# Lower halves of 18 of h's tiles made by TensorE and ScalarE, and another order of work from the sweep's last column to the table of ids

## The chip, the cores and the metric

One core of a Trainium2 chip runs the whole kernel. The metric is the device time of one execution in microseconds (us); the time before is the median of three runs. PE is TensorE (PEld its weight loads), DVE VectorE, ACT ScalarE, POOL GpSimd, SP the engine that only issues transfers.

## The reference

x has 6250 nodes of 256 numbers, and there are 200,000 edges, sorted by their destination. Cut to what matters:

```
deg_out, deg_in = edges per source, edges per destination (at least 1)
h = x * rsqrt(deg_out)
m = segment_sum(h[src], dst) * rsqrt(deg_in)
y = m @ W_gc + b_gc + x @ W_res + b_res
logits = y @ Wg + bg;  the two largest of 64 experts, gates = softmax of the two
per expert: gelu(tokens @ w1 + b1) @ w2 + b2, times the gate, added to y
batch norm over the nodes, added to x, layer norm per node
```

## The kernel before

**Making h.** The source nodes stand in 49 tiles of 128 (hrow). TensorE projects each tile by W_gc first, so that h has 256 columns of x @ W_gc, times the scale s_out of its node. Products of the sweep are done in f32r (one pass), so each row of h is kept in two halves: upper(t) has ScalarE write the scaled row, rounded to f32r, into the tile's first 256 columns; lower(t) has VectorE write what the rounding left, old * s_out - upper, over the unscaled row in the second 256. Each call takes the tiles t-1 and t, t odd. Behind every fourth or sixth tile lower(t) has SP write a block of tiles (512 columns each) to memory as h_dram: the blocks end with the tiles 5, 9, 15, 19, 25, 29, 35, 39, 45 and 48.

**The edge sweep.** The first 1118 groups of 128 edges are taken densely: for each of 30 windows of 128 destination nodes, TensorE counts edges per source and destination (count, L859: one-hot lo of the source by one-hot hotk of the destination, both made by VectorE), ScalarE and VectorE put the counts into SBUF (L879, L902), and multiply (L914, L915) multiplies the counts with the 49 tiles of hrow. The other 445 groups are gathered: GpSimd fetches 128 rows of h_dram by an indirect transfer (fetch, L768) into a ring of 8 buffers, and TensorE adds them by one-hot products (L773, L774). A plan written in advance (dense(), a list of costs) sets the program order: counts of the next window and gathers stand between the multiplies at set distances, and each engine keeps that order. In the opening, 40 groups of the first window are counted with a call of halves(t) after every four; the calls for t = 29 to 49 stand in the first window's multiplies, two tiles apart.

**The sweep's end.** The gathered windows are done before the last dense one, and the last of their results overhangs into the last dense window. last_rows() (L923 to L928) brings it there: after the last multiply ScalarE scales the sum by okc into res (L918), TensorE makes the overhang's product (L926), VectorE adds it (L927), and the ACT queue writes res into z_dram. Meanwhile VectorE works off choices_until(), pieces of the routing of the nodes that are done.

**Routing.** The last three tiles of nodes are loaded from z_dram, finished and sent through the gate; VectorE then ranks each choice within its expert, and TensorE's and VectorE's table() turns the ranks into lists of token ids per expert, by which rows of x are gathered for the experts. busy(n) is n products of TensorE whose result nobody reads. Order is by hand here: `ranks(1, ...)`, then the difference of the two best logits (g2), busy(8), the experts' counts and places (L1479 to L1494, with TensorE's transposition L1486 and product L1487 of them), the table's factors. softmax (L1280) turns g2 into gates: ScalarE's Exp and a copy plus 1, VectorE's reciprocal and two more.

Of the kernel before, what the change touches and what calls it, by code (L numbers as in the profile page):

```python
# [26 lines left out]
TP = 125  # L27
# [23 lines left out]
PAIRS = 8  # L51
MARGIN = 48


# [120 lines left out]
def gnn_moe_kernel(ctx, tc, x_in, x_cols, src, dst, bases, nexts, firsts, parts, lasts, W_gc, b_gc, W_res, b_res, Wg, bg, w1, b1, w2, b2,  # L175
# [9 lines left out]
    def node_rows(ap, t0, n):  # L185
        return ap[t0 * TP:(t0 + n) * TP, :].rearrange("(t p) d -> p t d", p=TP)

    def source_out(tile_ap, ap, t0, n):

        whole = min(n, NS - 1 - t0)  # L190
        if whole > 0:
            nc.sync.dma_start(out=ap[t0 * SP:(t0 + whole) * SP, :].rearrange("(t p) d -> p t d", p=SP),
                              in_=tile_ap[:, :whole, :])
        if t0 + n >= NS:
            for a, b in ((0, 96), (96, ODD)):
                nc.sync.dma_start(out=ap[(NS - 1) * SP + a:(NS - 1) * SP + b, :], in_=tile_ap[a:b, NS - 1 - t0, :])
# [24 lines left out]
    def f32(ap):  # L221
        return ap.bitcast(F32)
# [128 lines left out]
    with tc.tile_pool(name="edges", bufs=1) as ep, ExitStack() as later:  # L351
# [50 lines left out]
        def upper(t):  # L402
            for u in range(t - 1, min(t + 1, NS)):
                S.activation(hrow[:, u, :D], f32(hrow[:, u, D:2 * D]), AF.Copy, scale=s_out[:, u:u + 1])

        def lower(t):
            at = range(t - 1, min(t + 1, NS))
            for u in at:
                V.scalar_tensor_tensor(hrow[:, u, D:2 * D], f32(hrow[:, u, D:2 * D]), s_out[:, u:u + 1],
                                       f32(hrow[:, u, :D]), op0=ALU.mult, op1=ALU.subtract)  # L410
            if t % 5 == 4 or t % 10 == 5:
                n = 6 if t % 10 == 5 else 4
                n -= max(t + 1 - NS, 0)
                t0 = at[-1] + 1 - n
                source_out(f32(hrow[:, t0:t0 + n, :2 * D]), h_dram, t0, n)

        def halves(t):
            upper(t)
            lower(t)

        with tc.tile_pool(name="late", bufs=1) as lp, tc.tile_pool(name="both", bufs=2) as bp, \
# [326 lines left out]
        with tc.tile_pool(name="xs", bufs=1) as xs, tc.tile_pool(name="hotg", bufs=2) as hg, \  # L748
# [6 lines left out]
            for i in range(2):  # L755
                for t0 in range(0, NS, 10):
                    G.memset(f32(counts[i][:, t0:min(t0 + 10, NS), :]), 0.0)

            NR = 8
            ring = []  # L760
# [150 lines left out]
            def multiply(c, t):  # L911

                sm, by = banks[c % 2][:, :D + 2], counts[c % 2][:, t, :]
                T.matmul(sm, by, hrow[:, t, D:], start=(t == 0), stop=False)  # L914
                T.matmul(sm[:, :D], by, hrow[:, t, :D], start=False, stop=(t == NS - 1))  # L915
                if t == NS - 1:
                    res = rsp.tile([WIN, D + 2], F32, name="resd")
                    S.activation(res, sm, AF.Copy, scale=okc[:, c:c + 1])  # L918
                    ends_met["dense"] = res
                    if c < ND - 1:  # L920
                        sums_done(res, c)

            def last_rows():  # L923

                pw, res = banks[(ND - 1) % 2][:, :D + 2], ends_met["dense"]
                T.matmul(pw, live["overd"], ends_met["gather"], start=True, stop=True)  # L926
                V.tensor_tensor(res, pw, res, ALU.add)  # L927
                sums_done(res, ND - 1, ACT_E, nc.scalar)  # L928

# [126 lines left out]
            def dense():  # L1056
# [21 lines left out]
                for c in range(ND):  # L1078
# [10 lines left out]
                    for t in range(NS):  # L1089
# [14 lines left out]
                        if c == ND - 1:  # L1104
                            if t == NS - 6:
                                yield 0.0, lambda: live.update(overd=rows_of(ND, "overd"))
                            yield 0.0, lambda t=t: choices_until(0.25 * t)

# [35 lines left out]
            def gather(n):  # L1144
                i, g = rows[n]
                g0, k = GATHER[i]
                if g == g0:
                    live["pg"] = ps_g.tile([WIN, D + 2], F32, name="pg")
                hot, further = batch.pop(n)
# [32 lines left out]
            for n in range(n, len(rows)):  # L1182
                gather(n)
            last_rows()
            choices_until(1e9)
# [93 lines left out]

    def softmax(g1, g2):  # L1280
        S.activation(g2, g2, AF.Exp)
        S.activation(g1, g2, AF.Copy, bias=1.0)
        V.reciprocal(g1, g1)
        V.tensor_mul(gates[:, :, 1], g2, g1)
        V.tensor_copy(gates[:, :, 0], g1)
# [18 lines left out]
    with tc.tile_pool(name="ps_r", bufs=1, space=PSUM) as ps_r, tc.manual_schedule():  # L1304
# [4 lines left out]
        brow = rt.tile([E, H + D], F32, name="brow")  # L1309
        nc.sync.dma_start(out=brow[:, :H], in_=b1)  # L1310
        nc.sync.dma_start(out=brow[:, H:], in_=b2)
        for t0 in range(ta, tb, 4):
# [6 lines left out]
        for t0 in range(0, NL, 4):  # L1319
            n = min(4, NL - t0)  # L1320
            node_dma(nc.sync, True, z[:, t0:t0 + n, :], node_rows(z_dram, ta + t0, n))
        pick[1] = [rt.tile([TP, E, NB], BF16, name=f"pick{j}") for j in range(2)]
        both[1] = rt.tile([TP, E, NB], BF16, name="both")
# [153 lines left out]
        V.tensor_sub(g2, top[:, :, 1], top[:, :, 0])  # L1477
        busy(8)
        V.tensor_copy(own, cps[:E, 3, 1:2])  # L1479
# [345 lines left out]
    with tc.For_i(0, n_again, 1), tc.tile_pool(name="all", bufs=1) as ap, \  # L1825
# [115 lines left out]
        g2 = ap.tile([TP, NT], F32, name="g2")  # L1941
        V.tensor_sub(g2, top[:, :, 1], top[:, :, 0])
        softmax(g1, g2)
        nc.sync.dma_start(out=node_rows(x_dram[:, D:], 0, NT), in_=gates)
# [236 lines left out]
```

## Time and profile before

| | us |
|---|---|
| runs | 1441.87, 1441.97, 1438.64 (median 1441.87) |
| profiled execution | 1442.04 |
| its span in the trace | 1440.4 |
| busy: TensorE, VectorE, ScalarE, GpSimd | 1334.3 (93%), 1079.3 (75%), 803.4 (56%), 758.1 (53%) |

The span in 40 slices of 36 us; a digit is the busy share in tenths, PEclk the clock that TensorE was granted, in tenths of 2.4 GHz, DMA the share of the 16 DMA engines:

```
PE   8999578999999999999999998799999999999683
DVE  9999889999989888777777768655555555544588
ACT  7898646577776666656555532533333333333358
POOL 6000337777667776766777643255465556565100
PEclk9999699999999999999999999899999999999897
DMA  6667676777778787778788764789788888687645
```

Slice 5 (144 to 180 us) is the end of the projections and the opening of the sweep, slices 25 and 26 (864 to 936 us) hold the sweep's end and the routing. Behind them come the 64 experts, and from about 1340 us the norms.

### The profile page before, as it was taken

How to read it: one execution, taken by the hardware profiler on the slowest of the kernel's cores; microseconds unless marked ns; L12 is line 12 of the kernel's file. 1: busy time of each engine (PE TensorE's matmuls, PEld its weight loads, DVE VectorE, ACT ScalarE, POOL GpSimd, SP SyncE). 2: the span in 40 equal slices, each digit the busy share in tenths (PEclk: the TensorE clock that was granted, in tenths of full speed). 3: DMA queues.
4: the chain of work that ended last, by engine and by line, in shares of the span. 5: the costliest groups of instructions: out<-in, count | busy, mean ns of one | idle time of the engine just before them, and what ended most of it. 6: DMA issues, size and time to landing. Idle time of an engine off the chain costs nothing. (4 is left out here: it accounts for less than half of the span.)

```text
span 1440.4 us, 32497 instructions
## 1 busy us (share of the span) xinstructions
PE 1334.3 (93%) x9814; PEld 1121.1 (78%) x9814; DVE 1079.3 (75%) x3326; ACT 803.4 (56%) x2127; POOL 758.1 (53%) x894
## 2 busy tenths in 40 slices
PE   8999578999999999999999998799999999999683
PEld 4555367888889999999999996688788998799441
DVE  9999889999989888777777768655555555544588
ACT  7898646577776666656555532533333333333358
POOL 6000337777667776766777643255465556565100
PEclk9999699999999999999999999899999999999897
DMA  6667676777778787788778764789788888687645
GB/s 213 192 206 221 223 244 180 208 227 217 206 223 228 211 234 221 216 227 228 218 214 229 208 189 137 170 237 300 258 274 280 257 253 261 212 266 237 248 142 168
DMA packets 198010, 319.89 MB, mean 222 GB/s; under 512 B 27345, under 2 KB 129595, under 8 KB 197826
## 3 DMA queue, kind: packets, MB, share of 16 engines
q1 hardware_dynamic: 149716, 170.68, 38.2%
q0 software_dynamic: 47888, 146.88, 35.4%
q8 instruction: 79, 1.29, 0.4%
q14 instruction: 105, 0.86, 0.2%
q10 hardware_dynamic: 222, 0.19, 0.0%
HBM read 250.84 MB, written 60.35 MB: 216 GB/s over the span
## 5 line engine op out<-in xcount | busy, mean ns | idle before, releaser
L768 POOL DMA_INDIRECT r<-h_dram,srcg x445 | 470.5, 1057 | 215.9 <-PE pc L859 70.6
L914 PE MATMUL sm<-hrow,room 128*128 128x258 f32 x1470 | 486.8, 346 | 5.2 <-DVE room L902 5.0
L879 ACT CAST room<-pc 128x196 f32 (+7 forms) x879 | 356.5, 406 | 163.2 <-PE pc L859 125.2
L915 PE MATMUL sm<-hrow,room 128*128 128x256 f32 x1470 | 394.7, 282 | 0.0
L859 PE MATMUL pc<-hotk,lo 128*128 128x245 bf16 (+7 forms) x1118 | 302.6, 303 | 24.0 <-DVE lo L386 12.9
L837 DVE TENSOR_TENSOR hotk<-key,iota_h 128x784 bf16<-128x784 f16 (+4 forms) x488 | 247.8, 508 | 96.1 <-PE pc L859 91.3
L914 PEld LDWEIGHTS sm<-hrow,room 128*128 128x128 f32 x1470 | 287.5, 196 | 12.4 <-issue 7.3
L915 PEld LDWEIGHTS sm<-hrow,room 128*128 128x128 f32 x1470 | 279.7, 190 | 1.2
L1674 ACT ACTIVATE hT<-ph,bc 128x112 f32<-128x112 f32 (+16 forms) x256 | 108.3, 427 | 257.9 <-PE ph L1672 252.7
L902 DVE TENSOR_TENSOR room<-pc,room 128x49 f32 x908 | 197.5, 240 | 12.5 <-ACT room L879 5.5
L1672 PE MATMUL ph<-xgT,w1s 128*128 128x112 f32 (+17 forms) x1024 | 201.5, 341 | 0.5 <-DVE xgT L1655 0.4
L1630 POOL DMA_INDIRECT y_dram<-ys,dest x124 | 120.0, 968 | 138.9 <-ACT ys L1726 100.1
L1672 PEld LDWEIGHTS ph<-xgT,w1s 128*128 128x128 f32 x1024 | 166.8, 193 | 20.1 <-issue 2.3
L1630 POOL DMA_INDIRECT xg<-x_dram,ids x124 | 120.4, 971 | 62.5 <-DMA w1s<-in_L_gnn_w_dram 21.4
L859 PEld LDWEIGHTS <-lo 128*128 128x128 bf16 x1118 | 97.9, 100 | 62.6 <-DVE lo L386 14.3
L773 PE MATMUL pg<-r,hot 128*128 128x258 f32 x445 | 143.2, 322 | 3.5 <-DMA r<-h_dram,srcg 1.8
L774 PE MATMUL pg<-r,hot 128*128 128x256 f32 x445 | 125.2, 281 | 0.0
L1688 PE MATMUL py<-w2s,hT 128*128 128x256 f32 (+3 forms) x424 | 103.0, 386 | 0.9 <-DVE y_sum L1727 0.9
L1655 DVE TENSOR_SCALAR xgT<-pte,bsum 128x112 f32<-128x112 f32 (+14 forms) x128 | 48.7, 422 | 70.2 <-PE pte L1652 69.8
L611 PE MATMUL pr<-room,f 128*128 128x512 f32 x196 | 99.6, 633 | 0.0
L1710 PE MATMUL ph<-hT,w2s 128*128 128x208 f32 (+9 forms) x480 | 98.1, 358 | 0.0
L386 DVE TENSOR_TENSOR lo<-lo_b,iota 128x1024 bf16<-128x1024 bf16 x140 | 95.9, 685 | 0.0
(374 smaller groups left out, 1942.6 us busy)
## 6 DMA issues: line engine op xcount, KB each, us to landing
w1s<-in_L_gnn_w_dram SPq DMA_DIRECT2D x64, 512.0 KB
w2s<-in_L_gnn_w_dram SPq DMA_DIRECT2D x64, 512.0 KB
yr<-y_dram SPq DMA_DIRECT2D x10, 1024.0 KB
h_dram<-hrow SPq DMA_DIRECT2D x5, 1536.0 KB
r<-h_dram,srcg POOLq DMA_INDIRECT x445
f<-in_x_cols_dram SPq DMA_DIRECT2D x25, 256.0 KB
z_dram<-zeros SPq DMA_DIRECT2D x7, 903.0 KB
r_dram<-hx SPq DMA_DIRECT2D x24, 256.0 KB
```

The lines of the kernel that those rows point to most:

```text
L768: G.indirect_dma_start(out=f32(r[:, :2 * D]), out_offset=None, in_=h_dram[:, :], in_offset=bass.IndirectOffsetOnAxis(ap=idx, axis=0))
L773: T.matmul(pg, hot, r[:, D:], start=first, stop=False)
L774: T.matmul(pg[:, :D], hot, r[:, :D], start=False, stop=last)
L837: V.tensor_tensor(hot, pairs(key, e, n, m), iota_h[:, None, :m, :].to_broadcast([128, n // 2, m, 2]), ALU.is_equal)
L859: T.matmul(pc, los[g // PAIRS][:, r // 2, :, r % 2], hots.pop(g), start=(i == 0), stop=(i == k - 1))
L879: put = S.copy(counts[c % 2][:, :, 1:][:, :, ds(at, w - 1)], pc[:, :, 1:])
L902: add = V.tensor_tensor(to, more, f32(had), ALU.add).ins
L914: T.matmul(sm, by, hrow[:, t, D:], start=(t == 0), stop=False)
L915: T.matmul(sm[:, :D], by, hrow[:, t, :D], start=False, stop=(t == NS - 1))
L1630: w = G.indirect_dma_start(**kw)
L1672: T.matmul(ph[:, :m], w1s[:, kk, c * 128:(c + 1) * 128], xgT[:, kk, :m], start=(kk == 0), stop=(kk == 1))
L1674: S.activation(hT[:, c, :m], ph[:, :m], AF.Gelu, bias=b1_e[:, c:c + 1])
```

## The change

- Every odd tile from 5 to 39 (18 of them, TURNED) gets its lower half in another way. lower(t) has ScalarE make a diagonal matrix of the tile's scales (the identity times s_out, two buffers). At the next call of halves, TensorE multiplies it with the unscaled rows (f32, into half of a PSUM bank) and subtracts the upper half with a product by the constant -1 diagonal (f32r). At the call behind that, ScalarE copies the result to the lower half. The write of a block waits until none of its tiles is under way (rows_to_dram). The bank is the one that the gathers use later.
- The overhang's product (met_rows) is made three tiles before the sweep's end into the other sum bank, and ScalarE copies it to SBUF. After the last multiply one VectorE instruction, sum * okc + overhang, takes the place of ScalarE's scaling, the product and the addition.
- The loads of b1 and b2 (128 and 64 KB) are issued behind those of z_dram's last rows and not ahead of r_dram's.
- Exp and the copy plus 1 (powers) are issued behind `ranks(1, ...)`, ahead of the counts; the rest of softmax stays. busy(8) there becomes busy(2).

```diff
+TURNED = range(5, 40, 2)
...
+        ahead, outs, low = [], [], {}
+
+        def by_products():
+            for u, done in list(ahead):
+                at = low["bank"][:, u // 2 % 2 * D:u // 2 % 2 * D + D]
+                if done:
+                    S.activation(hrow[:, u, D:2 * D], at, AF.Copy)
+                    ahead.remove((u, done))
+                else:
+                    T.matmul(at, low.pop(u), f32(hrow[:, u, D:2 * D]), start=True, stop=False)
+                    T.matmul(at, low["less"], hrow[:, u, :D], start=False, stop=True)
+                    ahead[ahead.index((u, done))] = (u, True)
+
+        def rows_to_dram():
+            while outs and all(u >= sum(outs[0]) for u, done in ahead):
+                t0, n = outs.pop(0)
+                source_out(f32(hrow[:, t0:t0 + n, :2 * D]), h_dram, t0, n)
+
         def lower(t):
             at = range(t - 1, min(t + 1, NS))
             for u in at:
+                if u in TURNED:
+                    low[u] = low["pool"].tile([128, 128], F32, name="scales", bufs=2)
+                    S.activation(low[u], ident, AF.Copy, scale=s_out[:, u:u + 1])
+                    ahead.append((u, False))
+                    continue
                 V.scalar_tensor_tensor(hrow[:, u, D:2 * D], f32(hrow[:, u, D:2 * D]), s_out[:, u:u + 1],
                                        f32(hrow[:, u, :D]), op0=ALU.mult, op1=ALU.subtract)
             if t % 5 == 4 or t % 10 == 5:
...
-                source_out(f32(hrow[:, t0:t0 + n, :2 * D]), h_dram, t0, n)
+                outs.append((t0, n))
+            rows_to_dram()
 
         def halves(t):
+            by_products()
             upper(t)
             lower(t)
...
+            low["pool"] = xs
+            low["bank"] = ps_g.tile([128, 2 * D], F32, name="pg")
+            low["less"] = xs.tile([128, 128], F32R, name="less")
+            S.activation(low["less"], ident, AF.Copy, scale=-1.0)
...
                     res = rsp.tile([WIN, D + 2], F32, name="resd")
-                    S.activation(res, sm, AF.Copy, scale=okc[:, c:c + 1])
-                    ends_met["dense"] = res
                     if c < ND - 1:
+                        S.activation(res, sm, AF.Copy, scale=okc[:, c:c + 1])
                         sums_done(res, c)
-
-            def last_rows():
-
-                pw, res = banks[(ND - 1) % 2][:, :D + 2], ends_met["dense"]
+                    else:
+                        V.scalar_tensor_tensor(res, sm, okc[:, c:c + 1], live["met"], op0=ALU.mult, op1=ALU.add)
+                        sums_done(res, c, ACT_E, nc.scalar)
+
+            def met_rows():
+                assert made["gathered"] == 0
+                met = xs.tile([128, 4 * TP], F32, name="xT", bufs=1)[:, :D + 2]
+                pw = banks[ND % 2][:, 512 - (D + 2):]
                 T.matmul(pw, live["overd"], ends_met["gather"], start=True, stop=True)
-                V.tensor_tensor(res, pw, res, ALU.add)
-                sums_done(res, ND - 1, ACT_E, nc.scalar)
+                S.copy(met, pw)
+                live["met"] = met
...
+                            if t == NS - 3:
+                                yield 0.0, met_rows
...
-            last_rows()
...
-    def softmax(g1, g2):
+    def powers(g1, g2):
         S.activation(g2, g2, AF.Exp)
         S.activation(g1, g2, AF.Copy, bias=1.0)
+
+    def softmax(g1, g2):
         V.reciprocal(g1, g1)
...
-        nc.sync.dma_start(out=brow[:, :H], in_=b1)
-        nc.sync.dma_start(out=brow[:, H:], in_=b2)
         for t0 in range(ta, tb, 4):
             n = min(4, tb - t0)
             node_dma(nc.sync, True, x(t0, n), node_rows(r_dram, t0, n))
...
             node_dma(nc.sync, True, z[:, t0:t0 + n, :], node_rows(z_dram, ta + t0, n))
+        nc.sync.dma_start(out=brow[:, :H], in_=b1)
+        nc.sync.dma_start(out=brow[:, H:], in_=b2)
...
         V.tensor_sub(g2, top[:, :, 1], top[:, :, 0])
-        busy(8)
+        powers(g1, g2)
+        busy(2)
```

## Rows read from the trace of the kernel before

**Rows 1.** Stretches: us, busy us (instructions) by engine, granted clock, DMA share, GB/s.
```profile
155.00:175.00 20.00, 5.58 (x45) 3.40 (x43) 19.03 (x49) 14.47 (x42) 7.18 (x23) 0.67 0.82 302
```
**Rows 2.** VectorE in order of time: start us, us, engine, line, operation, how many.
```profile
165.07 0.60 DVE L837 TENSOR_TENSOR hotk<-key,iota_h 128x882 bf16<-128x882 f16 x1
165.60 0.86 DVE L409 SCALAR_TENSOR_TENSOR hrow<-hrow,s_out 128x256 fp32r<-128x256 f32 x2
...
168.07 0.60 DVE L837 TENSOR_TENSOR hotk<-key,iota_h 128x882 bf16<-128x882 f16 x1
...
181.58 0.88 DVE L409 SCALAR_TENSOR_TENSOR hrow<-hrow,s_out 128x256 fp32r<-128x256 f32 x2
```
**Rows 3.** GpSimd in order of time, the first gather; in brackets its wait.
```profile
199.02 1.09 POOL L768 DMA_INDIRECT r<-h_dram,srcg  x1 [35.91 <-DMA h_dram<-hrow]
```
**Rows 4.** Stretches of the writes of h, with all engines.
```profile
181.80:183.40 1.60, 1.54 (x15) 1.29 (x13) 1.60 (x6) 1.43 (x5) 0.00 (x0) 1.00 0.02 6
183.40:196.70 13.30, 8.87 (x54) 7.23 (x52) 11.89 (x34) 6.50 (x23) 0.00 (x0) 0.74 1.01 369
```
**Rows 5.** Stretches, the gathers of line 768 alone: GpSimd, clock, DMA.
```profile
199.00:287.00 88.00, 69.52 (x60) 1.00 0.68 193
```
**Rows 6.** Waits of TensorE, 250 to 300 us: total us, times, longest.
```profile
PE pg L773 <- DMA r<-h_dram,srcg: 1.8, 2, 0.9
```
**Rows 7.** ScalarE in order of time, a call of halves in the opening.
```profile
159.50 0.91 ACT L404 ACTIVATE hrow<-hrow,s_out 128x256 fp32r<-128x256 f32 x2
160.31 0.23 ACT L879 CAST room<-pc 128x49 f32 x1
160.39 0.52 ACT L404 ACTIVATE hrow<-hrow,s_out 128x256 fp32r<-128x256 f32 x1
```
**Rows 8.** Groups by line, whole span: count, busy us, mean ns, idle before.
```profile
L1162 ACT COPY resg<-pg 128x258 f32<-128x258 f32 x28 | 10.5, 376 | 12.4 <-PE pg L1160 11.5 <-PE pg L774 0.6 <-issue 0.3
L1137 ACT CAST hot<-thin 128x128 fp32r<-128x128 bf16 x44 | 10.2, 295 | 14.4 <-DVE thin L386 14.3
```
**Rows 9.** TensorE in order of time, f32 products of 256 columns (experts).
```profile
931.56 1.96 PE L1688 MATMUL py<-w2s,hT 128*128 128x256 f32 x8
```
**Rows 10.** TensorE in order of time, the sweep's last products.
```profile
869.86 0.28 PE L914 MATMUL sm<-hrow,room 128*128 128x258 f32 x1
869.98 0.28 PE L915 MATMUL sm<-hrow,room 128*128 128x256 f32 x1
870.83 0.70 PE L926 MATMUL sm<-resg,overd 128*128 128x258 f32 x2 [0.57 <-ACT resd L918]
```
**Rows 11.** VectorE in order of time, the same moment.
```profile
871.02 0.53 DVE L343 TENSOR_TENSOR room<-room 125x704 bf16<-125x704 bf16 x1
871.57 0.43 DVE L927 TENSOR_TENSOR resd<-sm,resd 128x258 f32<-128x258 f32 x1
```
**Rows 12.** Waits, 869 to 925 us: total us, times, longest.
```profile
DVE s_in L1417 <- DMA room<-z_dram: 1.3, 1, 1.3
```
**Rows 13.** VectorE in order of time, the experts' places.
```profile
890.06 0.07 DVE L1483 DVE_READ_ACCUMULATOR scr<-haves,place,ones 64x1 f32 x1
...
892.71 0.29 DVE L1493 CAST place_b<-cps 125x128 f16<-125x128 f32 x1 [1.45 <-PE cps L1487]
```
**Rows 14.** TensorE in order of time, the same stretch.
```profile
889.44 2.56 PE L1398 MATMUL acc_c<-room 125*125 125x352 bf16 x8
891.92 0.37 PE L1486 MATMUL cps<-ident,first_b 64*128 64x64 f32 x1
```
**Rows 15.** ScalarE in order of time, ahead of the gates.
```profile
898.57 1.28 ACT L1281 ACT_TABLE_LOAD   x1
```
**Rows 16.** VectorE in order of time, the gates.
```profile
900.41 0.47 DVE L1283 RECIPROCAL g<-g 125x50 f32<-125x50 f32 x1 [0.25 <-ACT g L1282]
```
**Rows 17.** Stretch of 1 us, TensorE alone: busy us, clock, DMA share, GB/s.
```profile
891.00:892.00 1.00, 1.00 (x5) 0.50 1.09 345
```

More of the change, by code (lines that the diff above doesn't have):

```diff
@@ L414, in lower @@
                 t0 = at[-1] + 1 - n
-                source_out(f32(hrow[:, t0:t0 + n, :2 * D]), h_dram, t0, n)
+                outs.append((t0, n))
+            rows_to_dram()
         def halves(t):
+            by_products()
             upper(t)
             lower(t)
+            assert t < NS - 1 or not ahead
         with tc.tile_pool(name="late", bufs=1) as lp, tc.tile_pool(name="both", bufs=2) as bp, \
@@ L1147, in gather @@
                 if g == g0:
-                    live["pg"] = ps_g.tile([WIN, D + 2], F32, name="pg")
+                    live["pg"] = ps_g.tile([WIN, 2 * D], F32, name="pg")[:, :D + 2]
                 hot, further = batch.pop(n)
@@ L1942, in gnn_moe_kernel @@
         V.tensor_sub(g2, top[:, :, 1], top[:, :, 0])
+        powers(g1, g2)
         softmax(g1, g2)
```

## The prediction, made before the changed kernel ran

> **What bounds the kernel now.** By the page's table of engines TensorE is nearly full, so a change to VectorE's work counts only where TensorE isn't. The 40 slices show two such stretches that the change touches: the opening of the edge sweep and the routing behind it. The table by stretches is next: from 155 to 175 us TensorE works 5.6 of 20 us, at 0.67 of its clock, and VectorE 19.0 [rows 1]. The order of VectorE's instructions says on what: one period of the opening, from one one-hot instruction to the next, is 3.00 us and holds two calls of halves, with four lower halves, 0.86 us a pair [rows 2]. So VectorE paces the making of h, at 1.50 us a call.
>
> It is tempting to stop there, but GpSimd's order names a second bound. Its first row gather waits 35.9 us, for the last write of h to memory, and starts at 199.0 us [rows 3]. These writes fill the DMA engines at 369 GB/s to 196.7 us; the one sizeable hole, 181.8 to 183.4, is one in which no block was ready [rows 4]. From then on GpSimd is full: between 199 and 287 us it starts 60 gathers, 69.5 us busy; with the 0.30 us that it stands between two of them that is 87.5 of 88 [rows 5]. And TensorE waits there for gathered rows, 1.8 us [rows 6]. So at 287 us the sweep stands where this rigid chain lets it: landing of h plus 60 gathers. A sweep that comes sooner waits longer; only h landing at another time, or a sweep later by over some 2 us, moves that point. Behind it TensorE is full to the sweep's end and again in the experts, so a shift there, or in the routing, goes through to the end.
>
> **Lower halves.** VectorE loses 18 instructions, 18 x 0.43 = 7.7 us. For each of them ScalarE gets a scaled identity (128x128) and a copy of 256 columns out of PSUM, TensorE an f32 and an f32r product.
>
> ScalarE's old work in a call is two upper halves, which the next instruction follows after 0.81 us, and half of the period's two count copies, 0.08 us each to the next start: 0.89 us at most [rows 7]. The nearest row to the new copy is the 258-column one, 0.38 us, some 0.10 less back to back (two of 0.52 us end after 0.91) [rows 7, 8]. A scaled identity is not in the trace; it lies between the 128x128 cast, 0.29 alone and 0.20 in a run, and the 256-column one with a scale, 0.40 [rows 7, 8]; I take 0.28. Sum: 0.89 + 0.28 + 0.28 = 1.45 us back to back, 1.55 if the copy starts from a wait; bounds 1.35 and 1.70. I take 1.50. So ScalarE takes VectorE's place at the same pace, and VectorE's 7.7 us become waiting: it can't run ahead, since the even tile's lower half needs the upper half that ScalarE makes in the same call. The Trainium skill (ScalarE: Activation LUTs, What ACT_TABLE_LOAD costs) gives 186 ns and 0.83 ns a column, 93 ns more for a scale by pointer, 93 ns of overlap: estimates of 0.31 and 0.29 us for the two, by which the sum would be 1.49.
>
> TensorE's f32 product of 256 columns is two instructions of 0.245 us, the f32r one follows at 0.12: 0.61 us, at the lower clock up to 1.22 [rows 9, 10]. With a call's four counts that fits into 1.50 us at 2.4 GHz and about fills it at 1.2. Free while the clock holds; up to 0.2 us a call if not.
>
> What moves is the landing of h: a block of tiles now waits for its last odd tile, whose copy stands two calls later at the head of ScalarE's work. ScalarE was in the call of tile 9 at 159.5 us [rows 7]; two scaled identities and the constant -1 one put that to 160.3. The block that ends with tile 35, the one behind the hole, is then ready 15 calls later: 160.3 + 15 x 1.50 + 0.33 = 183.1 us. Before, VectorE had its last pair done at 182.46 [rows 2]. The shift is +0.7 us, and the 13.3 us of full DMA behind it hand it on to the first gather. At 1.35 us a call it is -1.6, though the holes allow no more than -0.8 (below), at 1.70 +3.7. I take +0.7. The blocks are alone in SP's queue then, and the PSUM bank is the gathers', whose first product comes later.
>
> **Sweep's end to ids.** The chain was: last matmul done at 870.26, ScalarE's scaling, the f32 product of the overhanging rows (0.70 us), VectorE's addition, done at 872.00 [rows 10, 11]. Now the product stands three tiles ahead of the end, and one VectorE instruction scales and adds. That looks like a cut of over 1 us, but VectorE was not free: an addition of the choices ran to 871.55, and that of res began at 871.57 [rows 11]. The new instruction stands behind the same choices and is about as long. Gain 0.0; bounds +0.6, if the choices come earlier, and -0.3, for the product between TensorE's last tiles. GpSimd's constants waited for ScalarE's scaling, the last reader of okc, and now wait for VectorE's instruction; all that they can hold up is ranking, which VectorE's wait for z hides.
>
> b1 and b2 (192 KB) behind z instead of ahead: they shared the engines with the write of res for which z's load waits. Only VectorE's wait for z, 1.3 us, can be gained [rows 12]. I take 0.4, bounds 0 and 0.8. They are read behind the last tiles' choices, long after.
>
> Six fillers less: the eight took 2.56 us, and the transposition behind them started at 891.92 though its operand was there at 890.13. VectorE waited 1.45 us for it, from 891.26 on [rows 13, 14]. Two fillers, 0.64 us at the rate of the eight, let the transposition and the product behind it end near 891.0, before VectorE is free. Gain 1.45 us; bounds 0 (third rival) and 1.45.
>
> The exponential ahead: its table load, 1.28 us, moves to where ScalarE waits for the counts, and VectorE's reciprocal no longer waits 0.25 us [rows 15, 16]. With the gap ahead of the reciprocal I take 0.35, bounds 0.2 and 0.4.
>
> **Sum.** +0.7 - 0.0 - 0.4 - 1.45 - 0.35 = -1.5 us. The profiled execution took 1442.04 us (span 1440.4), 0.17 above the median of the runs, 1441.87; on that the forecast is 1440.4 us, and the rivals below count from it too.
>
> **Clock.** Under the eight fillers the granted clock was 0.50 with TensorE always busy [rows 17]. The Trainium skill (TensorE: Matmul & The Clock Gate, Part 1) calls the throttled state the default, which activity releases. By that rule less filling can hold the lower level longer; no row here shows the leaner stretch, so it is the third rival.
>
> **Rivals.**
> 1. Faster: the hole of 1.6 us closes, since the calls take 1.45 us or less and the products keep the clock up. The blocks start 0.8 later, so h lands 0.8 sooner; with 0.8 for b1 and b2, 1.45 and 0.4 that is -3.45, 1438.4 us, and 1437.0 where the choices also gain 0.6 and the sweep 0.8. For it: TensorE idles through most of the opening. Against: ScalarE's sum.
> 2. Slower: ScalarE and TensorE in lock-step. The copy waits for a product, the product for ScalarE's identity, the next count copy for counts queued behind that product. At 1.8 us a call tile 35 is ready at 187.6, 5.2 us late; less 2.2 that is +3.0, 1444.9 us; at 1.9, 1446.3. It decides from 1.6 us a call, where h's loss passes the gain behind the sweep. For it: at the lower clock TensorE fills a call. Against: five count banks and two identities let each run somewhat ahead.
> 3. The clock stays low behind the fillers: the products of the places outlast VectorE and the 1.45 us are lost, 1441.8 us.
> 4. The first gather is not held by h's last write, or not the sweep by the gathers: VectorE's 7.7 us come through, within TensorE's 14 idle us. Then 1441.9 - 7.7 - 2.2 = 1432.0 us. The wait of 35.9 us speaks against it.
>
> **How the numbers follow.** Forecast 0.47, rival 1 0.22, rival 2 0.18, rival 3 0.09, rival 4 0.04. A measurement of this kernel can tell 0.3% (4.3 us) from no change. Faster by that, below 1437.5: half of rival 1, rival 4, a little of the forecast: 0.2. Slower by that, above 1446.2: some two thirds of rival 2, at 1.9 us and more a call: 0.12. Within it 0.68. The range, 8 in 10, is 1436.5 to 1445.5; the forecast's own is 1439.0 to 1442.5.
>
> **What would show it.** Right: 31 lower halves on VectorE, which idles for ScalarE in the opening; a first gather between 199 and 201; GpSimd as full to 287 us as before, with TensorE waiting longer for rows; the write of res no nearer to the last tile's choices; no wait of VectorE for the transposed counts and no table load behind them. Wrong: a first gather before 198, a sweep that ends 3 us sooner, calls above 1.6 us, or the clock at its lower level through the places.

## The result: slower, 1467.16 us

Forecast 1440.4 us. Measured: median 1467.16 us (1462.20 to 1467.49, five runs) against 1441.87 (1438.64 to 1444.58, five runs): ratio 1.0174, 95% interval 1.0160 to 1.0187. The profiled execution has a span of 1465.7 us, before 1440.4: +25.3 us.

| | before | after |
|---|---|---|
| first write of h issued | 159.69 | 163.20 |
| first gather | 199.02 | 223.57 (+24.55) |
| 9th, 61st, 201st, 441st gather | 210.20, 287.27, 489.90, 843.01 | +26.05, +26.40, +27.13, +27.12 |
| last product of the sweep starts | 869.98 | 897.68 (+27.70) |
| from there to the end of the span | 570.4 | 568.0 (-2.4) |

So the loss is complete when the gathers start, and goes to the end nearly as it is; behind the sweep the sum comes near the forecast's, though its pieces do not (below). First, GpSimd's order at its first gather [rows 3]:

```profile
start us, us, engine line op out<-in xcount [idle before <-releaser]
223.57 1.31 POOL L799 DMA_INDIRECT r<-h_dram,srcg  x1 [61.54 <-DMA h_dram<-hrow]
```

It waits for h 25.6 us longer. The stretch of the opening [rows 1]:

```profile
core 0: us, PE busy (x) PEld busy (x) DVE busy (x) ACT busy (x) POOL busy (x), PEclk, DMA share, GB/s
155.00:175.00 20.00, 11.06 (x43) 7.03 (x42) 9.90 (x23) 11.99 (x38) 7.03 (x23) 0.59 0.46 170
```

TensorE works twice as long as before, at a lower clock, VectorE half as long, and the DMA engines are at 0.46. No engine is full: engines wait for each other. Of before's VectorE period [rows 2] this is left, one call of halves on all engines (TensorE's weight loads left out):

```profile
165.11 0.24 ACT L910 CAST room<-pc 128x49 f32 x1 [0.85 <-PE pc L890]
165.20 0.39 ACT L413 ACTIVATE hrow<-pg 128x256 fp32r<-128x256 f32 x1
165.48 0.91 ACT L405 ACTIVATE hrow<-hrow,s_out 128x256 fp32r<-128x256 f32 x2
165.65 1.22 PE L416 MATMUL pg<-hrow,scales 128*128 128x256 f32 x2 [0.63 <-ACT hrow L413]
166.02 0.48 DVE L433 SCALAR_TENSOR_TENSOR hrow<-hrow,s_out 128x256 fp32r<-128x256 f32 x1 [0.40 <-ACT hrow L405]
166.27 0.40 ACT L430 ACTIVATE scales<-ident,s_out 128x128 f32<-128x128 f32 x1
166.31 0.78 PE L417 MATMUL pg<-hrow,less 128*128 128x256 f32 x1
...
166.88 0.55 PE L890 MATMUL pc<-hotk,lo 128*128 128x98 bf16 x4
167.53 0.24 ACT L910 CAST room<-pc 128x49 f32 x1 [0.86 <-PE pc L890]
167.62 0.39 ACT L413 ACTIVATE hrow<-pg 128x256 fp32r<-128x256 f32 x1
...
168.07 1.22 PE L416 MATMUL pg<-hrow,scales 128*128 128x256 f32 x2 [0.63 <-ACT hrow L413]
```

Read it as a ring. ScalarE's copy of a tile starts (165.20); 0.45 us later the f32 product of the next tile starts, which waited for that copy though it writes the other half of the bank; the two products take 1.23 us, the four counts behind them 0.65; then ScalarE's copy of the counts, and 0.09 us later, behind it in ScalarE's order, the copy of that tile (167.62). Once round is 2.42 us. TensorE's part of it is long too: the two products take 1.23 us from the first's start to the counts, and 0.66 in two_banks below, where the granted clock is 1.00 (2.4 GHz). Here it is 0.50 (1.2 GHz) from 158.8 to 213.4 us; the table by stretches in the middle of that:

```profile
175.00:190.00 15.00, 11.61 (x44) 8.02 (x44) 7.21 (x18) 9.31 (x30) 0.00 (x0) 0.50 0.60 230
```

In the first window four multiplies come into the ring, mostly 3.36 us a call. The waits of 155 to 215 us say the same (engine and line, what it waited for, us in total, times, the longest):

```profile
DVE hrow L433 <- ACT hrow L405: 21.6, 18, 2.8
ACT room L910 <- PE pc L890: 19.5, 17, 2.0
PEld pg L416 <- ACT hrow L413: 15.9, 17, 1.5
PE pg L416 <- ACT hrow L413: 11.4, 17, 1.2
...
ACT less L789 <- DMA hrow<-hx: 2.9, 1, 2.9
```

17 of the 18 products wait for the copy before. The last line is another cost: ScalarE stands 2.9 us ahead of making the constant -1 identity, for the transfer of projected rows (hx), which by this releaser still reads the place where the constant lies.

The Trainium skill (PSUM — Partial Sum Buffer, PSUM bank collisions raise a hardware error) says that two engines may not use one PSUM bank in the same partitions at the same time, whatever the addresses, and that a program's semaphores are to guard PSUM by bank and not by address. The trace agrees: TensorE's write to one half waits for ScalarE's read of the other, 17 times of 18. This rule speaks against the change, and the forecast didn't weigh it. The runs don't tell whether the wait hangs on the bank or on the tile of the program that fills it, since two_banks below gives each half a tile and a bank of its own.

### The profile page after: what moved, and what is told of

The parts are those of the page before. It is cut to its first block, busy times and chain, and to the rows that moved or that the text cites. A ratio compares the mean times of both kernels' runs of the same rounds, so it can differ in the third digit from the quotient of the medians.

```text
span 1465.7 us, 32612 instructions
## 1 busy us (share of the span) xinstructions
PE 1359.4 (93%) x9862; PEld 1138.7 (78%) x9862; DVE 1074.6 (73%) x3308; ACT 815.6 (56%) x2164; POOL 756.1 (52%) x894
```

## The experiments

Openings start at slightly different times from execution to execution (after: TensorE's clock over 150 to 155 us was 0.80, before 0.50), so the landing of h is counted from ScalarE's first upper halves (four in one row) to the first gather. ScalarE's order in the kernel before, and in the changed one:

```profile
155.70 1.71 ACT L404 ACTIVATE hrow<-hrow,s_out 128x256 fp32r<-128x256 f32 x4
```

```profile
154.14 1.71 ACT L405 ACTIVATE hrow<-hrow,s_out 128x256 fp32r<-128x256 f32 x4
```

With [rows 3] that is 199.02 - 155.70 = 43.32 us, and 223.57 - 154.14 = 69.43: the loss is 26.1 us, 1.56 of it covered by an earlier start. For all kernels (ratios to the kernel before on the same chip, whose median is in the last column):

| kernel | starts | first gather | landing | ratio, 95% interval | before |
|---|---|---|---|---|---|
| before | 155.70 | 199.02 | 43.32 | | |
| the change | 154.14 | 223.57 | 69.43 | 1.0174 (1.0160 to 1.0187) | 1442 |
| early_only | 156.26 | 224.59 | 68.33 | 1.0154 (1.0118 to 1.0190) | 1547 |
| gap_filled | 155.94 | 210.99 | 55.05 | 1.0107 (1.0072 to 1.0141) | 1530 |
| gap_filled_early | 155.92 | 210.34 | 54.42 | 1.0089 (1.0060 to 1.0117) | 1547 |
| copy_first | 155.47 | 208.48 | 53.01 | 1.0103 (1.0061 to 1.0145) | 1530 |
| two_banks | 154.80 | 204.75 | 49.95 | 1.0090 (1.0056 to 1.0124) | 1529 |
| two_banks_early | 154.73 | 203.66 | 48.93 | 1.0039 (1.0014 to 1.0065) | 1530 |
| nine_tiles | 155.96 | 205.81 | 49.85 | 1.0045 (1.0025 to 1.0064) | 1547 |
| doubled | 155.68 | 210.38 | 54.70 | 1.0059 (1.0041 to 1.0076) | 1442 |
| dead_products | 155.49 | 201.87 | 46.38 | 1.0030 (1.0007 to 1.0054) | 1529 |
| ends_only | 154.84 | 200.99 | 46.15 | 1.0022 (1.0004 to 1.0040) | 1529 |
| left_out | 155.22 | 198.95 | 43.73 | | |
| five_tiles | 154.12 | 197.61 | 43.49 | 0.9973 (0.9963 to 0.9983) | 1442 |
| three_tiles | 155.40 | 197.97 | 42.57 | 0.9997 (0.9983 to 1.0010) | 1442 |
| ends_clean | 155.82 | 199.14 | 43.32 | 0.9992 (0.9970 to 1.0014) | 1530 |
| eight_fillers | 155.73 | 199.05 | 43.32 | 0.9993 (0.9978 to 1.0007) | 1442 |

The chips differ (last section), so landings are compared across them and whole times only within one. The kernel before and the two that have neither turned tiles nor the constant (ends_clean, eight_fillers) land at 43.32, to the hundredth, where the whole takes 1440 us and where it takes 1528.

**ends_only: the way behind the sweep alone.**

```
-TURNED = range(5, 40, 2)
+TURNED = ()
```

> The lower halves all on VectorE again, the new way behind the sweep kept. If the loss lies only in the making of h: first gather of rows within 0.3 us of 199.0, the stretch from the sweep's last product to the end as in the changed kernel, 2.1 us shorter than before (570.1 to 568.0 us), so 1441.9 - 2.1 = 1439.8 us. Rival, that part of the loss is behind the making of h (the product of the overhanging rows among the last tiles, or the later writes): first gather at 199, but 1441.5 us or more.

The landing is not as before but 2.8 us later. ScalarE's order names it:

```profile
154.84 1.71 ACT L405 ACTIVATE hrow<-hrow,s_out 128x256 fp32r<-128x256 f32 x4
156.45 0.56 ACT L645 COPY hx<-pr 128x512 f32<-128x512 f32 x1
159.92 0.31 ACT L789 ACTIVATE less<-ident 128x128 fp32r<-128x128 f32 x1 [2.91 <-DMA hrow<-hx]
```

The constant is still made, and holds the next upper halves until the transfer of hx is done.

**two_banks.**

```
-at = low["bank"][:, u // 2 % 2 * D:u // 2 % 2 * D + D]
+at = low["bank"][u // 2 % 2][:, :D]          # the gathers' bank, and the second window's
```

> The two places for the products lie in two PSUM banks, not in two halves of one. Theory (the shared bank ties TensorE's next product to ScalarE's copy of the tile before, with the counts between them): the wait for that copy goes, a call of the opening takes what TensorE needs at 1.2 GHz, 0.66 + 0.57 + 0.62 = 1.85 us instead of 2.42, and one of the first window 2.69 instead of 3.37; 13 x 0.57 + 8 x 0.68 = 12.8 us come back, 1454 us; if TensorE without gaps is granted 2.4 GHz as well, ScalarE's 1.55 us sets the call, and 25 us come back, 1442. Rival (ScalarE's order, the count's copy ahead of the tile's copy, makes the lock-step, whatever the bank): 2.3 us a call or more, 1464 us or more.

The landing comes back by 19.5 us of 26.1. A call takes 1.45 us in the opening, and the clock is up from 166.4 us on. All engines in the opening, weight loads left out, and a stretch:

```profile
168.24 0.24 ACT L911 CAST room<-pc 128x49 f32 x1
168.32 0.40 ACT L413 ACTIVATE hrow<-sm 128x256 fp32r<-128x256 f32 x1
168.39 0.70 PE L416 MATMUL pg<-hrow,scales 128*128 128x256 f32 x2 [0.88 <-ACT scales L430]
168.59 0.91 ACT L405 ACTIVATE hrow<-hrow,s_out 128x256 fp32r<-128x256 f32 x2
168.74 0.47 PE L417 MATMUL pg<-hrow,less 128*128 128x256 f32 x1
169.05 0.36 PE L891 MATMUL pc<-hotk,lo 128*128 128x98 bf16 x4
...
169.39 0.41 ACT L430 ACTIVATE scales<-ident,s_out 128x128 f32<-128x128 f32 x1
...
169.68 0.25 ACT L911 CAST room<-pc 128x49 f32 x1
```

```profile
175.00:190.00 15.00, 11.52 (x81) 9.10 (x78) 10.48 (x26) 13.65 (x45) 0.00 (x0) 1.00 0.81 303
```

(The second is the table by stretches; ScalarE is the fourth engine, the granted clock the third number from the end.) No product waits for a copy; ScalarE goes from one round to the next without a gap, 0.08 + 0.27 + 0.80 + 0.29 = 1.44 us. That is the forecast's sum back to back (0.89 + 0.28 + 0.28). The whole is 13.8 us slower than before on this chip (8.6 to 19.0), more than the 6.6 us of landing explain: in the profiled executions, 7.4 us lie behind the start of the sweep's last product (611.5 us to the end, 604.1 in ends_only), where both run the same code. two_banks_early's 5.6 us of landing below are 6.0 us of the whole.

**left_out and dead_products: the room, and the load.** left_out has nothing in place of the 18 lower halves. dead_products keeps VectorE's, and does products that nobody reads:

```
+T.matmul(at, ident, f32(hrow[:, 1, D:2 * D]), start=True, stop=False)
+T.matmul(at, low["less"], hrow[:, 1, :D], start=False, stop=True)
```

> The lower halves of the 18 tiles are left out altogether (those columns keep what they held), with nothing on TensorE and ScalarE in their place: what the change could at best give. Theory (h's writes fill the DMA engines, and gathers follow at their own pace): VectorE needs 2.14 instead of 3.00 us for two calls, but h lands at most 1.6 us sooner, the hole closed; first gather 197.4 to 199.0, 1439.8 less 0 to 1.6: 1438.2 to 1439.8 us. Rival (VectorE's 7.7 us come through to the end): 1432 us.

> VectorE makes all lower halves as before; TensorE does 18 pairs of products of the same size at the same places in its order, on a finished tile, and nobody reads them: TensorE's load without the ties. By the ties alone (theory): VectorE sets the call at 1.50 us again, first gather at 199 to 201 us, 1440 to 1442 us. By TensorE's load at 1.2 GHz alone (rival): its 1.85 us a call in the opening and 2.69 in the first window hold the counts, and through them VectorE; first gather at 205 us or later, 1448 us or more.

Both still make the constant, so ends_only is their measure. left_out lands 2.4 us sooner than that: all that VectorE's 7.7 us can be worth here. (Its h is not right, its later stages work on other data, and the whole takes 13036 us; only its opening is read.) dead_products lands 0.23 us later: TensorE's added products cost next to nothing by themselves. What cost 26 us is ScalarE's added work and, above all, how it and the products are tied.

**ends_clean and two_banks_early: without the constant's wait.**

```
-low["less"] = xs.tile([128, 128], F32R, name="less")
+low["less"] = ep.tile([128, 128], F32R, name="less")    # made earlier; in ends_clean not at all
```

> All lower halves on VectorE and the constant -1 identity gone too; only the new way behind the sweep is left. Theory: ScalarE's wait of 2.9 us for the transfer of hx, which it had in the changed kernel and with the ends alone (it makes the constant in a place that this transfer still reads), goes; the first write of h is issued at 159.7 us again and not at 161.7, the first gather starts 2.0 us sooner than with the ends alone, at 199.0, and the whole is 2.1 us faster than the kernel before (ratio 0.9985). Rival (that wait was hidden behind the transfers, and the ends alone are what lost): first write at 159.7, first gather at 201 all the same, ratio 1.000 or more.

> Two PSUM banks for the products, and the constant -1 identity made earlier, in a place of its own. Theory: ScalarE sets the call at 1.45 us as with two banks alone, the start comes back by 2.0 us; first gather at 204.75 - 2.0 = 202.7 us, 3.7 us later than before, less 2.1 us behind the sweep: ratio 1.001. Rival (the start is hidden, the landing follows from ScalarE's work alone): first gather at 204.5, ratio 1.002 or more.

ends_clean lands at 43.32 as before: the wait was 2.8 us of landing. With two banks only 1.0 us comes back, for the first scaled identity then waits for the same transfer, 2.1 us. What is left, 5.6 us: the first write is issued 7.98 us behind the start, before 3.99; the rest are calls of 1.5 to 2.3 us in the first window.

**gap_filled: one bank, and dead products in the gaps.**

```
+for n in range(3):
+    T.matmul(low["spare"][:, :D], low["less"], hrow[:, 1, :D], start=True, stop=True)
 T.matmul(at, low.pop(u), f32(hrow[:, u, D:2 * D]), start=True, stop=False)
```

> One bank with two halves as in the changed kernel; ahead of each f32 product TensorE does three dead products of 256 columns into the other window's bank, 0.64 us at 1.2 GHz, as long as the gap in which it waits for ScalarE's copy. Theory (the gaps that the tie leaves keep the granted clock at 0.50, and half of the loss is that): the clock rises to 1.0 within some us, a call takes copy 0.45 + products 0.65 + counts 0.36 + the count's copy 0.15 = 1.6 us in the opening and 2.0 in the first window; first gather at 203 to 206 us, 1446 to 1449 us by the first comparison's chip. Rival (the tie alone makes the 2.42 us, or dead products lengthen the loop): clock 0.50, 2.4 us a call or more, first gather at 223 us or later, 1467 us or more.

One turn of the ring, and the same stretch:

```profile
170.60 0.39 ACT L413 ACTIVATE hrow<-pg 128x256 fp32r<-128x256 f32 x1
170.88 0.91 ACT L405 ACTIVATE hrow<-hrow,s_out 128x256 fp32r<-128x256 f32 x2
171.05 0.70 PE L418 MATMUL pg<-hrow,scales 128*128 128x256 f32 x2 [0.21 <-ACT hrow L413]
171.40 0.46 PE L419 MATMUL pg<-hrow,less 128*128 128x256 f32 x1
...
171.70 0.37 PE L893 MATMUL pc<-hotk,lo 128*128 128x98 bf16 x4
...
171.89 0.60 PE L417 MATMUL sm<-hrow,less 128*128 128x256 f32 x3
172.16 0.25 ACT L913 CAST room<-pc 128x49 f32 x1
172.26 0.39 ACT L413 ACTIVATE hrow<-pg 128x256 fp32r<-128x256 f32 x1
```

```profile
175.00:190.00 15.00, 12.67 (x90) 10.11 (x88) 9.59 (x25) 12.46 (x41) 0.00 (x0) 1.00 0.87 325
```

The ring is the same, more work is in it, and it turns in 1.65 us, since the clock is 1.00: 14.4 us of landing for nothing but dead work (the first gather was expected 5 us sooner still; the first window takes 2.2 us a call, and the clock rose only at 168.1 us). That it is the clock, and not the filling by itself, is seen in the calls before that, TensorE's order:

```profile
162.58 1.22 PE L418 MATMUL pg<-hrow,scales 128*128 128x256 f32 x2 [0.20 <-ACT scales L432]
...
164.15 0.99 PE L417 MATMUL sm<-hrow,less 128*128 128x256 f32 x3
165.03 1.22 PE L418 MATMUL pg<-hrow,scales 128*128 128x256 f32 x2
```

At 0.50 and without a gap a call still took 2.45 us (and the next 2.41). So over half of the loss is the clock, which in the changed kernel stayed at 0.50 with TensorE at work for 63 to 89% of each 5 us and a gap of mostly 0.63 to 0.69 us in each call; the wait for the bank at the full clock is 5.1 us more (gap_filled to two_banks). The Trainium skill (TensorE: Matmul & The Clock Gate, A second HAM failure mode: psum-queue depth-cycling) tells of a kernel whose short idle times between groups of products take the clock down and up over and over. This case differs: with such gaps the clock stayed down for 55 us here, and in two_banks it stayed at 1.00 with a gap of 0.44 us in each call of 1.45. There it had risen at 166.4 us, behind calls with gaps of 0 to 0.19 us. Which gaps keep it down, no run shows.

**copy_first: the tile's copy ahead of the count's copy.**

```
+if g % 4 == 3:                     # and ahead of the counts in the first window
+    yield 0.0, lambda: copies()
 yield of_one_hots(0) / n, lambda g=g: count(g)
```

> One bank with two halves; ScalarE's copy of a tile is put ahead of the count's copy in its order, and so no longer waits for the four counts that TensorE does behind that tile's product. Theory (the tie costs this much only since the copy stands behind the counts; TensorE needs 1.85 us at 1.2 GHz without gaps): the wait for the copy before goes, the clock rises, ScalarE sets the call at 1.45 to 1.55 us; first gather at 203 to 206 us. Rival (the halves of one bank tie product and copy in any order): 2.0 us a call or more, first gather at 215 us or later.

In between: mostly 1.97 us a call while the clock was low (TensorE waits 0.18 us for the copy, the copy 0.33 for the product), about 1.45 once it rose at 172 us, 1.9 to 3.0 when it was at 0.50 again from 179 to 186, and 3.1 us later in landing than two banks. The order was a part of it, but not the whole.

**The last of the ring: gap_filled_early and early_only**, both with the constant made early.

> One bank, the gaps filled with dead products, and the constant made early. Theory (what the first gather gains passes to the end one to one while it is later than in the kernel before): granted clock 1.0 in the opening, 1.65 us a call, first gather at 209 to 210 us, 10 to 11 us later than before; where the kernel before takes 1442 us this one takes 1442 + 11 + 2.5 (the ninth gather's wait and what follows) - 2 = 1453 us, ratio 1.008. Rival (the low clock costs in the opening only, and the sweep takes up part of it): ratio 1.004 or less.

> The changed kernel with the constant -1 identity made early and nothing else. Theory (the tie at the low clock, not the start, is the loss): 2.42 and 3.36 us a call, granted clock 0.50, first gather 1 to 2 us sooner than in the changed kernel, at 221.5 to 222.6 us; ratio to the kernel before 1.016. Rival (the late start is what let the clock fall, TensorE having nothing to do for 5 us ahead of its first product): the clock comes up as with the gaps filled, first gather at 210 us, ratio 1.008.

early_only turns in 2.42 and 3.36 us at 0.50 as the changed kernel does, though TensorE's first product comes 1.1 us sooner behind the start (its wait is 4.36 us instead of 5.45). In two_banks that wait is 5.45 us as well, and the clock rose all the same: the late start is not what held it down. gap_filled_early's 11.1 us of landing appear in the whole as 0.0089 x 1547 = 13.8 us; 1.0089 where 1.008 was expected, and 1.004 or less by the rival: a later landing is not taken up by the sweep.

**Fewer tiles: five_tiles, three_tiles, nine_tiles.**

```
-TURNED = range(5, 40, 2)
+TURNED = (11, 13, 21, 23, 31)     # two banks; three_tiles: (11, 21, 31), one bank; nine_tiles: range(5, 40, 4), two banks
```

> Only five tiles' lower halves (11, 13, 21, 23, 31) by TensorE and ScalarE, with two PSUM banks and the constant -1 identity made early. Theory (ScalarE has room in the calls between, so VectorE's 5 x 0.43 = 2.1 us let the block of tile 35 be ready before its transfer's turn, and the hole of 1.6 us closes): first gather at 197.5 us against 199.1 with none of them, ratio to the kernel before 1 - (1.6 + 2.1) / 1529 = 0.9976. Rival (a tile whose copy comes two calls later holds its block by as much as VectorE gained): first gather at 199 us or later, ratio 0.9990 or more.

> Three tiles (11, 21, 31), five calls apart, by TensorE and ScalarE, with the two halves of one PSUM bank as in the changed kernel and the constant made early. Theory (the tie costs only between neighbours: here the copy before is long done): no wait of TensorE for a copy, VectorE 1.3 us ahead at tile 35, first gather at 197.9 us, ratio 0.9978. Rival (each product costs a call a lock-step, at the low clock near 1 us): first gather at 200 us or later, ratio 1.000 or more.

> Nine tiles (5, 9, 13, ... 37), every second call, with two banks and the constant made early. Theory (ScalarE's call takes 1.17 us on average, VectorE's 1.29, both below the 1.50 of before, so the transfers set the landing): first gather at 197.5 to 198.5 us; it reaches the end only in part, since the sweep stands at the same place from the 200th product on whether h lands at 197.6 or at 199; ratio 0.9975 to 0.9990. Rival (copies two calls late and waits between ScalarE and TensorE eat it): first gather at 200 us or later, ratio 1.000 or more.

Five tiles' first gather came when expected, for another reason: the opening began 1.3 to 1.6 us sooner than in the three others on this chip, and from its start the landing is 43.49, no gain. Three tiles gain 0.75 us of landing, and nothing that can be measured in the whole. five_tiles is nevertheless the one version that is measurably faster than the kernel before, 0.9973; with the way behind the sweep alone it was 0.9993 on the same chip, the intervals meet, and in the profiles the 441st gather starts at 842.69 and 842.74: what the tiles have to do with it stays open. Nine tiles are slower: the clock stays at 0.50 to 185 us, and the ring closes in another place, two calls in 3.50 us:

```profile
PE pg L418 <- ACT scales L432: 13.2, 8, 4.3
```

TensorE's product waits for the scaled identity (8 times of 9), the counts wait behind it, and ScalarE's next round waits for the counts.

**doubled: a later landing without TensorE or ScalarE.**

```
+if u in range(5, 40, 2):
+    V.scalar_tensor_tensor(low["dead"], f32(hrow[:, u, D:2 * D]), s_out[:, u:u + 1], f32(hrow[:, u, :D]), ...)
```

> All lower halves on VectorE; those of the 18 tiles are done once more by VectorE into a tile that nobody reads, 18 x 0.43 = 7.7 us more. Theory (VectorE paces the making of h, and a later landing goes through to the end, gather by gather): 1.93 us a call in the opening, first gather 6.9 to 7.7 us later, at 206 to 207 us, ratio to the kernel before 1 + (7.3 - 2.1) / 1529 = 1.0034. Rival (the sweep takes up a later landing, TensorE's idle us): first gather as late, ratio 1.000 or less.

A third instruction in a call costs 0.52 us, not 0.43 (two calls take 4.04 us where they took 3.00), and h lands 11.4 us later, more than expected; 18 x 0.52 is 9.4, and where the rest arises stays open. The 441st gather starts at 857.12, with the way behind the sweep alone (eight_fillers) at 842.74: +14.4. The whole is 8.5 us slower than before, some 9.5 slower than with the way behind the sweep alone; the profiled execution is 2.9 above its kernel's median. A later landing goes through.

**eight_fillers: the fillers again.**

```
-busy(2)
+busy(8)
```

> The new way behind the sweep alone, but with the eight filling products ahead of the transposed counts again. Theory (the two fillers give back most of what they win, since the 16 products behind the places then run at 1.2 GHz, 4.55 us instead of 3.45): VectorE waits 1.4 us for the transposed counts again, the 16 products take 3.45 us, and from z's arrival to the first product of the ids it takes 22.1 us, 0.4 more than in the changed kernel (21.72). Rival (the 16 products' clock has nothing to do with the fillers): they take 4.5 us as well, and it takes 23.2 us.

Neither came. The eight fillers ran at the full clock, there was no wait of VectorE for the transposed counts, and the places came 11.19 us behind z's arrival (881.07). TensorE's and VectorE's order, and one us of the table by stretches:

```profile
890.42 1.36 PE L1433 MATMUL acc_c<-room 125*125 125x352 bf16 x8
891.71 0.27 PE L1522 MATMUL cps<-ident,first_b 64*128 64x64 f32 x1
...
892.26 0.28 DVE L1529 CAST place_b<-cps 125x128 f16<-125x128 f32 x1
```

```profile
891.00:892.00 1.00, 1.00 (x9) 0.71 (x7) 0.93 (x6) 0.98 (x2) 0.00 (x0) 1.00 1.09 347
```

In the changed kernel TensorE's clock was low a little later, under the 16 products behind the places (VectorE's and TensorE's order, then one us of the table by stretches):

```profile
917.73 0.28 DVE L1531 CAST place_b<-cps 125x128 f16<-125x128 f32 x1
...
919.60 4.55 PE L1422 MATMUL acc_c<-tmp_c,unit_h 125*125 125x400 f16 x16 [0.85 <-DVE tmp_c L1410]
```

```profile
921.00:922.00 1.00, 1.00 (x5) 0.68 (x4) 1.00 (x3) 0.00 (x0) 0.00 (x0) 0.50 0.08 23
```

So the 2.56 us of the eight fillers [rows 14, 17] were some 3 us of low clock that lay there in that execution.

## Why the prediction was wrong, point by point

**The step that failed** is the call of halves: "So ScalarE takes VectorE's place at the same pace", 1.50 us, with rival 2's lock-step dismissed because "five count banks and two identities let each run somewhat ahead". The banks that mattered were not the counts' but the one of the products. Measured: 2.42 us in the opening, 3.36 in the first window, and a first gather 24.55 us later where +0.7 was forecast. Its 15 calls all had one price, though the last of them lie in the first window with its multiplies. The lock-step was rival 2's in kind, but with another wait in it: there the product waits for ScalarE's identity, here it waited for ScalarE's copy of the tile before. Its price, 1.8 to 1.9 us a call, and its chance, 0.18, were too low, since it did not count a ring in which the two engines stand one behind the other, at the low clock. The loss of 26.1 us of landing splits, with the pieces taken away in this order, into 14.4 us clock, 5.1 us the shared bank at the full clock, 1.0 us the constant's wait, and 5.6 us that two banks don't heal. So the step would have failed without the shared bank too: 5.6 us is still eight times the forecast's +0.7.

**ScalarE's sum** was right for what it counts: 1.45 us back to back, and 1.45 in two_banks where ScalarE has no gap.

**TensorE** "about fills" 1.50 us at 1.2 GHz: its 1.23 + 0.65 = 1.88 us are more than that, and "up to 0.2 us a call" was too little for the case that the clock does not hold. By itself its load cost 0.23 us of landing (dead_products); in the ring at 0.50 it was most of a call.

**The start.** "Two scaled identities and the constant -1 one put that to 160.3": the constant waited 2.9 us, and where it was made early the first identity waited 2.1, both for a transfer that still reads their places, which no list of costs shows.

**The rigid chain** holds to one side. A later landing goes through gather by gather, and grows a little (+24.55 at the first gather, +26.05 at the ninth, which waited 1.68 us for TensorE, +27.1 later). An earlier one does not: three_tiles' first gather was 1.05 us sooner than before's, its 61st at 287.18, before 287.27. So the 0.8 us that the first rival sets on an earlier landing were, by this run, not to be had.

**Sweep's end and z.** From the last product's start to z's first use 8.93 us, before 10.15 [rows 10, 12]: -1.2, forecast -0.0 and -0.4. Half of it is the new VectorE instruction: it starts 0.98 us behind the last product's start, where the addition started 1.59 behind [rows 10, 11], so the gain was the upper bound, 0.6, and not 0.0. VectorE's wait for z is 0.54 us instead of 1.28.

**Fillers and exponential.** From z to the places 11.12 us instead of 12.58: the 1.45 us of the forecast, and VectorE's reciprocal waits no longer. But from the places to the first product of the ids 10.60 instead of 9.94, the 16 products at the low clock taking 4.55 instead of 3.45. It was the third rival's loss in another place; and eight_fillers shows that the term itself was one execution's clock, not a cost of the fillers: z to ids takes 20.4 to 20.7 us with two or with eight when no low clock falls there.

**Sum behind the sweep**: -2.4 us from the last product's start to the end, forecast -2.2. That it fits is luck: to z it is -1.2 instead of -0.4, from z to the ids -0.8 instead of -1.8, and with the same way behind the sweep this stretch takes 568.7, 568.0 and 566.9 us in three_tiles, five_tiles and doubled, and 566.4 with eight fillers. In whole times the way behind the sweep alone is 0.9992 (0.9970 to 1.0014) with two fillers in ends_clean and 0.9993 (0.9978 to 1.0007) with eight: no gain that can be told from none.

## What to carry to other kernels

Before a step goes from one engine to a pair of engines, draw the ring: which buffer each of them waits for, what else stands in front of it in each order, and the sum once round at both clocks; count two halves of one PSUM bank as one buffer. Ask where every new tile lies, and what still reads that place. And before a duration is called the cost of an instruction, look at the granted clock over it and at a second execution: a term of 1.45 us can be a low clock that falls elsewhere next time.

## What the runs showed of the hardware that was not expected

- In the changed kernel the clock stayed at 0.50 from 158.8 to 213.4 us, with TensorE's products covering 63 to 89% of each 5 us from 160 to 210. With the gaps filled with dead work (gap_filled) it rose at 168.1 us, and h landed 14.4 us sooner.
- Chips differ by 6 to 7% for the same kernel: 1442, 1529 and 1547 us for the kernel before. The landings of the kernels without the change agree to the hundredth between the first two; the difference comes later: in ends_clean (chip of 1530 us) the first gather is at 199.14, as before, the 441st at 891.53, 48.5 us later, and from the first product of the ids to the end it takes 578.4 us instead of 537.7, 40.6 more. Why was not studied.
- VectorE's third lower half of a call costs 0.52 us in doubled, where a pair took 0.79 from its first start to the next instruction's (165.60 to 166.39). The delay lies ahead of the third, which writes over what the dead one reads: it starts 0.04 us after the dead one's end, while the others start 0.08 before the end of the one ahead of them.
